# A gated FFN with a masked product, all in fp32: its products done by Strassen's algorithm

## The chip, the cores and the metric

The kernel runs on one core of a Trainium2 chip. The metric is the device time of one execution in microseconds (us), the median of several runs. The engines are TensorE (PE in the profile; PEld is its weight load), VectorE (DVE), ScalarE (ACT), GpSimd (POOL) and SyncE (SP, which here only issues DMAs). Each engine runs its own list of instructions strictly in order and waits on semaphores of the others.

## The reference

There are 2048 tokens (2 x 1024) of 512 features, in fp32. xn is the layernorm of x over its features. The mask is 0 or 1 in blocks of 32 x 32, and a block of the weight is kept where the mask's sum over it is above 0.

```python
xn = _layernorm(x, axis=-1)
s = einsum('bsk,nk->bsn', xn, weight * block_mask)          # 512 x 512
nx = xn * rsqrt(mean(xn * xn) + 1e-5) * ln_w
g = einsum('bsh,ih->bsi', nx, gate_w)                       # 1792 x 512
u = einsum('bsh,ih->bsi', nx, up_w)                         # 1792 x 512
f = einsum('bsi,hi->bsh', silu(g) * u, down_w)              # 512 x 1792
out = x + s * silu(f)
```

## The kernel before

The main loop takes 4 blocks of TB = 512 tokens one after the other. Every product on TensorE is 128 x 128 weights by 128 x 512, in fp32; the profile counts each product written in the code as two instructions. 736 products are written: 224 for gate, 224 for up, 224 for down, 64 for the masked weight.

`prep` (L83 to L128) normalises a block token by token on VectorE (L95 to L113), transposes it on TensorE (L123) and evicts it twice, once times ln_w (L126, VectorE) and once plain (L127, ScalarE). `gate_up` (L143 to L162) then runs over 14 tiles f of the inner dimension: four products into one PSUM bank for gate (L149), four for up (L154), a silu out of PSUM on ScalarE (L158) and one multiplication on VectorE (L160), which makes a tile h that stays in SBUF. `finish` (L164 to L186) runs over 4 tiles of 128 tokens: 14 products with h as the weights of TensorE (L171), 4 of the masked product (L176), silu (L180), two operations on VectorE (L182, L185) and a store (L186). PSUM is accumulated over the contraction: a bank is read once in four, or once in fourteen, products.

All weights are loaded once by SP's queue at the start (L69 to L74) and stay in SBUF. A scheduler orders the instructions of each engine. GpSimd does nothing after it has made the identity matrix. In DRAM lie only inputs and the output.

## Time and profile before

| | |
|---|---|
| median of 3 runs | 658.58 us (658.03 to 659.58) |
| span of the profiled execution | 657.3 us |
| granted TensorE clock, mean | 0.998 |
| first product of gate starts | 12.25 us |
| transposes, 64 instructions of 128x128 (L123) | 10.4 us busy |
| up (L154) and masked product (L176), TensorE busy | 201.4 us and 57.5 us |
| statistics, 16 on VectorE (L95) | 675 ns each |
| eviction by ScalarE, 16 (L127) | 586 ns each |
| DMA over the span | 21.72 MB, 33 GB/s; 424 GB/s in the second of 40 slices |
| a 256 KB load of x, issue to landing | 3.9 us |
| a 256 KB store of the output, issue to landing | 2.0 us |

An engine's busy time alone does not tell what bounds the kernel; the chain of waits, which follows the last instruction back to what released it, does. In a line of a group stand: line, engine, operation, output <- inputs, shapes, count, busy time in us and mean duration in ns, and the idle time of the engine just before these instructions with what ended it. Durations of TensorE's instructions overlap, so they are read from starts. Starts in the timeline are us from the span's start.

### The profile page before, as it was taken

To read this page: it belongs to the slowest core of one execution; us is meant where nothing else is said; L and a number is where in the kernel's file an instruction comes from. 1 tells how busy PE (TensorE), PEld (TensorE's weight loads), DVE (VectorE), ACT (ScalarE), POOL (GpSimd) and SP (SyncE) were. 2 spreads that over 40 slices of the span, in tenths; PEclk is the share of its full clock that TensorE was granted. 3 is DMA by queue.
4 is the path that set the end of the run, shared out by engine and by line. 5 is a ranking of instruction groups with operands and counts; after the bars stand their busy time and mean duration, and the time that the engine had idled before them with its cause. 6 is when DMAs were issued, how large, how long until landed. Compare 5 with 4: busy or idle time off the path is not lost.

```text
span 657.3 us, 3624 instructions
## 1 busy us (share of the span) xinstructions
PE 642.3 (98%) x1538; PEld 288.0 (44%) x1538; DVE 102.0 (16%) x184; ACT 63.5 (10%) x100; POOL 0.7 (0%) x6
## 2 busy tenths in 40 slices
PE   3999999999999999999999999999999999999997
PEld 2444444444444444444444444444444444444442
DVE  5223012200140010200032100120001001010000
ACT  1211101100111001100011010010000000100000
POOL 0000000000000000000000000000000000000000
PEclk9999999999999999999999999999999999999999
DMA  9940000000100000000020000000000000000000
GB/s 324 424 179 0 0 1 0 2 31 16 52 29 0 0 0 1 0 16 17 16 80 1 0 0 1 0 0 17 16 16 16 1 0 0 1 0 0 25 24 16
DMA packets 7359, 21.72 MB, mean 33 GB/s; under 512 B 944, under 2 KB 944, under 8 KB 6832
## 3 DMA queue, kind: packets, MB, share of 16 engines
q1 hardware_dynamic: 7344, 21.50, 8.6%
q8 instruction: 12, 0.20, 0.1%
q14 instruction: 3, 0.02, 0.0%
HBM read 17.30 MB, written 4.19 MB: 33 GB/s over the span
## 4 chain that ended last, share of the span: by engine, by line
PE 98%; DVE 1%; DMA 1%; SPq 0%; issue 0%; ACT 0%; DVEq 0%
PE pg L149 29%; PE py L171 29%; PE pu L154 29%; PE pss L176 8%; PE pt L123 1%; DMA x<-in_x 1%; DVE st L95 0%; SPq L56 0%; DVE o L182 0%; DVE nxT L126 0%; DVE o L185 0%; DVE nz L113 0%; DVE agg L96 0%; ACT root L105 0%; DVE inv L107 0%
## 5 line engine op out<-in xcount | busy, mean ns | idle before, releaser
L149 PE MATMUL pg<-nxT,gate_sb 128*128 128x512 f32 x448 | 202.9, 595 | 0.6 <-DVE nxT L126 0.6
L154 PE MATMUL pu<-nxT,up_sb 128*128 128x512 f32 x448 | 201.4, 592 | 0.0
L171 PE MATMUL py<-down_sb,h 128*128 128x512 f32 x448 | 195.7, 592 | 0.0
L149 PEld LDWEIGHTS pg<-nxT,gate_sb 128*128 128x128 f32 x448 | 85.4, 191 | 107.3 <-issue 106.3
L154 PEld LDWEIGHTS pu<-nxT,up_sb 128*128 128x128 f32 x448 | 85.1, 190 | 107.1 <-issue 107.1
L171 PEld LDWEIGHTS py<-down_sb,h 128*128 128x128 f32 x448 | 84.5, 190 | 103.3 <-issue 103.3
L160 DVE TENSOR_TENSOR h<-sg,pu 128x512 f32<-128x512 f32 x56 | 38.5, 688 | 313.8 <-PE pu L154 313.8
L158 ACT ACTIVATE sg<-pg 128x512 f32<-128x512 f32 x56 | 33.5, 597 | 322.7 <-PE pg L149 322.5
L176 PE MATMUL pss<-w_sb,nzT 128*128 128x512 f32 x128 | 57.5, 592 | 0.0
L182 DVE SCALAR_TENSOR_TENSOR o<-pss,root,g 128x512 f32<-128x512 f32 x16 | 12.0, 751 | 218.5 <-PE pss L176 192.9
L176 PEld LDWEIGHTS pss<-w_sb,nzT 128*128 128x128 f32 x128 | 24.3, 190 | 30.6 <-issue 30.6
L180 ACT ACTIVATE g<-py 128x512 f32<-128x512 f32 x16 | 9.6, 597 | 216.9 <-PE py L171 216.9
L123 PE MATMUL pt<-ident,nz 128*128 128x128 f32 x64 | 10.4, 311 | 9.7 <-DVE nz L113 9.7
L123 PEld LDWEIGHTS pt<-ident,nz 128*128 128x128 f32 x64 | 8.7, 161 | 14.9 <-issue 12.3
L126 DVE TENSOR_SCALAR nxT<-pt,lnw_sb 128x512 f32<-128x512 f32 x16 | 11.4, 745 | 6.1 <-PE pt L123 6.0
L95 DVE BATCH_NORM_STATS2 st<-x 128x6 f32<-128x512 f32 x16 | 10.8, 675 | 9.7 <-DMA x<-in_x 9.7
L127 ACT COPY nzT<-pt 128x512 f32<-128x512 f32 x16 | 9.4, 586 | 25.8 <-DVE nxT L126 25.4
L185 DVE TENSOR_TENSOR o<-o,x 128x512 f32<-128x512 f32 x16 | 11.1, 692 | 0.5
L113 DVE TENSOR_SCALAR nz<-x,agg,scl 128x512 f32<-128x512 f32 x16 | 7.7, 541 | 0.1
L158 ACT ACT_TABLE_LOAD x4 | 5.1, 1283 | 1.6 <-PE pg L149 1.6
L105 ACT ACT_TABLE_LOAD x4 | 5.1, 1283 | 0.8 <-PEq L229 0.7
L96 DVE BATCH_NORM_AGGREGATE agg<-st 128x2 f32<-128x6 f32 x16 | 2.9, 181 | 0.4
(20 smaller groups left out, 11.9 us busy)
## 6 DMA issues: line engine op xcount, KB each, us to landing
x<-in_x SPq DMA_DIRECT2D x16, 256.0 KB, 3.9
out<-o SPq DMA_DIRECT2D x16, 256.0 KB, 2.0
gate_sb<-in_gate_t SPq DMA_DIRECT2D x7, 512.0 KB, 10.0
up_sb<-in_up_t SPq DMA_DIRECT2D x7, 512.0 KB, 10.2
down_sb<-in_down_t SPq DMA_DIRECT2D x2, 1792.0 KB, 17.1
mask_sb<-in_mask_t SPq DMA_DIRECT2D x1, 1024.0 KB, 11.4
w_sb<-in_w_t SPq DMA_DIRECT2D x1, 1024.0 KB, 12.6
lnw_sb<-in_ln_w SPq DMA_DIRECT2D x1, 2.0 KB, 4.0
```

The source lines that it names most:

```text
L95: nc.vector.bn_stats(st, xt[:, t, :])
L123: nc.tensor.transpose(pt[:, t * P : (t + 1) * P], nz[:, t, c * P : (c + 1) * P], ident)
L126: nc.vector.tensor_scalar_mul(nxT[:, c, :], pt, lnw_sb[:, c : c + 1])
L149: nc.tensor.matmul(pg, gate_sb[:, f, c, :], nxT[:, c, :], start=(c == 0), stop=(c == KC - 1))
L154: nc.tensor.matmul(pu, up_sb[:, f, c, :], nxT[:, c, :], start=(c == 0), stop=(c == KC - 1))
L158: nc.scalar.activation(sg, pg, AF.Silu)
L160: nc.vector.tensor_mul(h, sg, pu)
L171: nc.tensor.matmul(py, hs[f][:, tok], down_sb[:, f, :], start=(f == 0), stop=(f == FC - 1))
L176: nc.tensor.matmul(pss, nzT[:, c, tok], w_sb[:, c, :], start=(c == 0), stop=(c == KC - 1))
L180: nc.scalar.activation(g, py, AF.Silu)
L182: nc.vector.scalar_tensor_tensor(o, pss, root[:, TT + t : TT + t + 1], g, ALU.mult, ALU.mult)
L185: nc.vector.tensor_add(o, o, xt[:, t, :])
```

## The change

Strassen's algorithm, in the form with 7 products and 15 sums, replaces 8 products of blocks by 7. With the blocks of A (weights) as A11, A12, A21, A22 and those of B (tokens), the products are numbered 1 to 7; sums of A are named S (outer level) and s (inner level), sums of B T and t.

All 2048 tokens are taken at once, transposed, so that B is 4 x 4 tiles (4 of features by 4 of 512 tokens), A for one `group` is 4 x 4 tiles (two of gate and two of up over 4 of features). A group therefore stands for 64 products, and two levels make it 7 x 7 = 49. There are seven groups for gate and up, and an eighth (g == G) for the masked weight. The outer product q is an `instance`; it consists of 7 inner products. `OUTER = (1, 2, 3, 5, 6, 7, 4)` is their order. Inner product number i of instance j stands at position 7 j + 2 i, so that two instances are always interleaved and each position holds one product. Within an instance some products add into a bank of which a copy or sum was taken before (`start=first`): `snap` reads the bank and TensorE then adds to it, four positions later.

`snap`, `total` and `last` read PSUM after each single product. Where the instance has no earlier sum (q = 1, 3, 5) three snaps and the last are copies on ScalarE and three totals are sums on VectorE; in the others all seven are sums on VectorE. `pool_add` adds the outer sums on GpSimd in SBUF. `done` then runs silu on ScalarE in SBUF and the multiplication that makes h on VectorE, and stores h to DRAM. `sums_of_h` makes the four other blocks that the products of down need, 8 subtractions on VectorE with 8 stores, at position 8.5 of the next group. `inner_a` and `outer_a` make the sums of the weights on GpSimd, into three buffers tagged s and five tagged S; `scale_a` applies ln_w to the weights on ScalarE. The sums of the tokens, T and t, are made once, during the first group, half on VectorE and half on GpSimd (`outer_b`, `inner_b`), and stay in SBUF.

Down is one level: 7 outer products, each over 7 pairs of tiles, 28 products of 128x512 each, 196 in all; a bank is read once in 7 products. The blocks of h are read back from DRAM (`load_h`), 14 tiles of 256 KB for each of the seven, into a pool of 52 buffers shared with the weights of down (`load_d`, `outer_d`), the result of the masked product (also kept in DRAM) and x. Output and a second copy of x are transposed on the host.

`tc.manual_schedule()` keeps every engine's list in the order of the events, which are sorted by position. All DMAs are on SP's queue. Left out of the diff are the removed functions, which stand above, the token statistics (as before in their kind), the mask's reduction (one per quarter, VectorE) and the host's layouts.

```diff
-    ps_gu = ctx.enter_context(tc.tile_pool(name="ps_gu", bufs=4, space=bass.MemoryType.PSUM))
...
+    h_dram = tc.dram_tile([7, G, 2, P, W], F32, name="h_dram")
...
+    bpool = ctx.enter_context(tc.tile_pool(name="bpool", bufs=52))
+    apool = ctx.enter_context(tc.tile_pool(name="apool", bufs=8))
+    cpool = ctx.enter_context(tc.tile_pool(name="cpool", bufs=4))
+    ps = ctx.enter_context(tc.tile_pool(name="ps", bufs=1, space=bass.MemoryType.PSUM))
...
+    PSB = {"X": 3, "Y": 2, "Z": 2, "V": 1}
+    def bank(tag, name):
+        return ps.tile([P, W], F32, tag=tag, name=name, bufs=PSB[tag])
...
+    def transpose(t, c, tag):
+        pt = bank(tag, f"pt_{t}_{c}")
+        for i in range(TT):
+            nc.tensor.transpose(pt[:, i * P : (i + 1) * P], nzs[t][i][:, c * P : (c + 1) * P], ident)
+        r = t2k(bpool, "b", f"raw_{c}_{t}")
+        if c % 2:
+            nc.vector.tensor_copy(r, pt)
+        else:
+            nc.scalar.copy(r, pt)
+        raw[c, t] = r
...
+    def inner_b(q, m, eng):
+        b11, b12, b21, b22 = (bblk[q, k, n] for k in (0, 1) for n in (0, 1))
+        if m == 1:
+            bop[q, 1], bop[q, 2], bop[q, 3] = b11, b21, b22
+            return
+        o = t2k(bpool, "b", f"t{q}_{m}")
+        a, b = {
+            5: lambda: (b12, b11),
+            6: lambda: (b22, bop[q, 5]),
+            7: lambda: (b22, b12),
+            4: lambda: (b21, bop[q, 6]),
+        }[m]()
+        add(eng, o, a, b, ALU.subtract)
+        bop[q, m] = o
...
+    def load_a(g, R, K):
+        a = t2k(apool, "a", f"a{g}_{R}{K}")
+        nc.sync.dma_start(a, gu[g, R, K] if g < G else wm[R, K])
+        aq[g, R, K] = a
+    def scale_a(g, R, K):
+        for c in range(2):
+            v = aq[g, R, K][:, c * 256 : (c + 1) * 256]
+            nc.scalar.mul(v, v, lnw_sb[:, 2 * K + c : 2 * K + c + 1])
...
+    def mask_a(R, K):
+        v = aq[G, R, K].rearrange("p (b j) -> p b j", j=BLK)
+        k = keep[:, 2 * R + K, :].unsqueeze(2).to_broadcast([P, 16, BLK])
+        nc.gpsimd.tensor_tensor(v, v, k, ALU.mult)
+    ablk = {}
+    def outer_a(g, q, eng):
+        if q in (1, 2, 4):
+            ablk[g, q] = aq[(g,) + {1: (0, 0), 2: (0, 1), 4: (1, 1)}[q]]
+            return
+        o = t2k(apool, "S", f"S{g}_{q}", bufs=5)
+        a, b, op = {
+            5: lambda: (aq[g, 1, 0], aq[g, 1, 1], ALU.add),
+            6: lambda: (ablk[g, 5], aq[g, 0, 0], ALU.subtract),
+            7: lambda: (aq[g, 0, 0], aq[g, 1, 0], ALU.subtract),
+            3: lambda: (aq[g, 0, 1], ablk[g, 6], ALU.subtract),
+        }[q]()
+        add(eng, o, a, b, op)
+        ablk[g, q] = o
+    def inner_a(g, q, eng):
+        a = ablk[g, q]
+        a11, a21, a12, a22 = (a[:, i * P : (i + 1) * P] for i in range(4))
+        s = t2k(apool, "s", f"s{g}_{q}", bufs=3)
+        s1, s2, s3, s4 = (s[:, i * P : (i + 1) * P] for i in range(4))
+        add(eng, s1, a21, a22)
+        add(eng, s2, s1, a11, ALU.subtract)
+        add(eng, s3, a11, a21, ALU.subtract)
+        add(eng, s4, a12, s2, ALU.subtract)
+        aop[g, q] = {1: a11, 2: a12, 3: s4, 4: a22, 5: s1, 6: s2, 7: s3}
...
+    def instance(j, g, q, prior, dest):
...
+        def mm(m, tag, key, first):
+            def emit():
+                if first:
+                    st[key] = bank(tag, f"{key}_{j}")
+                nc.tensor.matmul(st[key], aop[g, q][m], bop[q, m], start=first, stop=True, skip_group_check=True)
+            return emit
+        def snap(key, name, i):
+            def emit():
+                s = t2k(cpool, name, f"{name}_{j}", bufs=2)
+                if prior is None:
+                    nc.scalar.copy(s, st[key])
+                else:
+                    add(nc.vector, s, st[key], prior(i))
+                st[name] = s
+            return emit
+        def total(key, name, i, after):
+            def emit():
+                add(nc.vector, dest(i), st[key], st[name])
+                after(i)
+            return emit
+        def last(key, i, after):
+            def emit():
+                if prior is None:
+                    nc.scalar.copy(dest(i), st[key])
+                else:
+                    add(nc.vector, dest(i), st[key], prior(i))
+                after(i)
+            return emit
+        def emit_all(after):
+            plan = (
+                (mm(1, "X", "x", True), snap("x", "s1", 0)),
+                (mm(5, "Y", "y", True), snap("y", "s5", 3)),
+                (mm(6, "X", "x", False), snap("x", "s2", 1)),
+                (mm(2, "Z", "z", True), total("z", "s1", 0, after)),
+                (mm(7, "X", "x", False), total("x", "s5", 3, after)),
+                (mm(3, "Y", "y", False), total("y", "s2", 1, after)),
+                (mm(4, "X", "x", False), last("x", 2, after)),
+            )
+            for i, (product, sums) in enumerate(plan):
+                at(7 * j + 2 * i, product)
+                at(7 * j + 2 * i + 0.5, sums)
+        return emit_all
+    def group(g):
+        base = 7 * 7 * g
...
+        def done(R, Hh, tiles):
+            def after(i):
+                if g == G:
+                    r, n = divmod(i, 2)
+                    t = 2 * Hh + n
+                    nc.gpsimd.tensor_tensor(tiles(i), tiles(i), rms_bc[:, t * W : (t + 1) * W], ALU.mult)
+                    nc.sync.dma_start(s_dram[2 * R + r, t], tiles(i))
+                    return
+                if i < 2:
+                    nc.scalar.activation(tiles(i), tiles(i), AF.Silu)
+                got.setdefault((R, Hh), set()).add(i)
+                for n in (0, 1):
+                    if {n, n + 2} <= got[R, Hh] and (R, Hh, n) not in hs:
+                        nc.vector.tensor_mul(tiles(n), tiles(n), tiles(n + 2))
+                        hs[R, Hh, n] = tiles(n)
+                        q = {(0, 0): 1, (1, 0): 2, (1, 1): 3}.get((R, Hh))
+                        if q:
+                            nc.sync.dma_start(h_dram[q - 1, g, n], tiles(n))
+            return after
+        got, hs = {}, {}
+        def sums_of_h(n):
+            b11, b21, b12, b22 = hs[0, 0, n], hs[1, 0, n], hs[0, 1, n], hs[1, 1, n]
+            T = {}
+            for q in (5, 7, 6, 4):
+                T[q] = t2k(cpool, "T", f"hT{g}_{n}_{q}", bufs=4)
+                a, b = {5: lambda: (b12, b11), 7: lambda: (b22, b12),
+                        6: lambda: (b22, T[5]), 4: lambda: (b21, T[6])}[q]()
+                add(nc.vector, T[q], a, b, ALU.subtract)
+                nc.sync.dma_start(h_dram[q - 1, g, n], T[q])
+        nothing = lambda i: None
+        def pool_add(dst, src):
+            return lambda i: add(nc.gpsimd, dst(i), dst(i), src(i))
+        def chain(*fs):
+            def after(i):
+                for f in fs:
+                    f(i)
+            return after
+        setup = {
+            1: (None, acc_, nothing),
+            2: (acc_, c1_, done(0, 0, c1_)),
+            3: (None, vc_, nothing),
+            5: (None, v5_, pool_add(vc_, v5_)),
+            6: (acc_, acc_, chain(pool_add(vc_, acc_), done(0, 1, vc_))),
+            7: (acc_, acc_, chain(pool_add(v5_, acc_), done(1, 1, v5_))),
+            4: (acc_, acc_, done(1, 0, acc_)),
+        }
...
+        for o, q in enumerate(OUTER):
+            prior, dest, after = setup[q]
+            instance(7 * g + o, g, q, prior, dest)(after)
+        if g < G:
+            at(base + 49 + 8.5, sums_of_h, 0)
+            at(base + 49 + 8.6, sums_of_h, 1)
...
+    def load_h(q):
+        for f in range(G):
+            for n in range(2):
+                hb[q, f, n] = t2k(bpool, "b", f"hb{q}_{f}{n}")
+                nc.sync.dma_start(hb[q, f, n], h_dram[q - 1, f, n])
...
+    def finish(R, Hh, i, y):
+        r, n = divmod(i, 2)
+        t, m = 2 * Hh + n, 2 * R + r
+        s, xx = fin[m, t]
+        nc.scalar.activation(y, y, AF.Silu)
+        nc.vector.tensor_mul(y, y, s)
+        nc.vector.tensor_add(y, y, xx)
+        nc.sync.dma_start(out_t[m * P : (m + 1) * P, t * W : (t + 1) * W], y)
...
+            def products(i=i, tag=tag, r=r, n=n):
+                b = bank(tag, f"py{q}_{i}")
+                for f in range(G):
+                    w = dop[q, f - f % 2][:, (f % 2) * 256 + r * P : (f % 2) * 256 + (r + 1) * P]
+                    nc.tensor.matmul(b, w, hb[q, f, n], start=(f == 0), stop=(f == G - 1))
+                A = lambda d, tag_: tile_of(d, tag_, i)
+                if q == 1:
+                    nc.scalar.copy(A(acc, "acc"), b)
+                elif q == 2:
+                    add(nc.vector, A(c1, "c1"), b, A(acc, "acc"))
+                    finish(0, 0, i, c1[i])
+                elif q == 3:
+                    nc.scalar.copy(A(vc, "vc"), b)
+                elif q == 5:
+                    nc.scalar.copy(A(v5, "v5"), b)
+                    add(nc.gpsimd, vc[i], vc[i], v5[i])
+                elif q == 6:
+                    add(nc.vector, acc[i], b, acc[i])
+                    add(nc.vector, vc[i], vc[i], acc[i])
+                    finish(0, 1, i, vc[i])
+                elif q == 7:
+                    add(nc.vector, acc[i], b, acc[i])
+                    add(nc.vector, v5[i], v5[i], acc[i])
+                    finish(1, 1, i, v5[i])
+                else:
+                    add(nc.vector, acc[i], b, acc[i])
+                    finish(1, 0, i, acc[i])
+            at(base + 28 * o + 7 * i, products)
...
+    at(NEG, load_x, 3)
+    tags = ("X", "Y", "Z", "X", "Y", "Z", "X", "V")
+    for t in (0, 1):
+        at(NEG + 1 + t, norm, t)
+        for c in range(KC):
+            at(NEG + 1 + t, transpose, t, c, tags[4 * t + c])
+    for R, K in QUADS:
+        at(NEG + 1.5, scale_a, 0, R, K)
+    for q in (1, 2):
+        at(NEG + 3, outer_a, 0, q, pool)
+        at(NEG + 3, inner_a, 0, q, pool)
+        for k in (0, 1):
+            for n in (0, 1):
+                at(NEG + 3, outer_b, q, k, n, dve)
+        for m in (1, 5, 6, 7, 4):
+            at(NEG + 3 + (q - 1), inner_b, q, m, dve)
+    at(0.6, norm, 2)
+    at(0.6, norm, 3)
+    for t in (2, 3):
+        for c in (2, 3, 0, 1):
+            at(1.2 + (t - 2) * 4 + 2 * ((c + 2) % 4) / 2, transpose, t, c, "V")
+    for q, pos in ((3, 9.6), (5, 14.6), (6, 21.6), (7, 28.6), (4, 35.6)):
+        for k in (0, 1):
+            for n in (0, 1):
+                at(pos + 0.1, outer_b, q, k, n, pool if (k + n) % 2 else dve)
+        for m in (1, 5, 6, 7, 4):
+            at(pos + 0.2, inner_b, q, m, dve if m in (5, 6, 4) else pool)
+    at(45.6, rms_factor)
+    for g in range(G + 1):
+        base = 49 * g
...
+        if g:
+            for R, K in QUADS:
+                at(base - 40, load_a, g, R, K)
+            for i, (R, K) in enumerate(QUADS):
+                if g < G:
+                    at(base - 24 + 2 * i + 0.7, scale_a, g, R, K)
+                else:
+                    at(base - 24 + 2 * i + 0.7, mask_a, R, K)
+            for q in (1, 2):
+                at(base - 15 + 7 * (q - 1) + 0.8, outer_a, g, q, pool)
+                at(base - 15 + 7 * (q - 1) + 0.9, inner_a, g, q, pool)
+        for i, q in enumerate((5, 6, 3, 7, 4)):
+            at(base - 7.1 + 2 * i, outer_a, g, q, pool)
+        for o, q in enumerate(OUTER[2:]):
+            at(base + 7 * o + 2.8, inner_a, g, q, pool)
+    for i, (R, K) in enumerate(QUADS):
+        at(49 * 4 + 6 * i + 0.75, mask_rows, R, K)
+    END = 49 * (G + 1) + 6
+    for i, (R, K) in enumerate(((0, 0), (1, 0), (1, 1), (0, 1))):
+        at(END - 14 + i, load_d, R, K)
+    for q in (1,):
+        at(END - 10, outer_d, q, pool)
+    for q in (2, 5, 6, 3, 7, 4):
+        at(END - 0.5, outer_d, q, pool)
+    at(END - 10, load_h, 1)
+    for o, q in enumerate(OUTER):
+        if o:
+            at(END + 28 * (o - 1) - 0.1, load_h, q)
+        quad = {2: (0, 0), 6: (0, 1), 7: (1, 1), 4: (1, 0)}.get(q)
+        if quad:
+            at(END + 28 * (o - 1) + 0.1, prefetch_out, *quad)
+        last_product(o, q, END)
...
+    with tc.manual_schedule():
+        for _, _, fn, args in sorted(events, key=lambda e: e[:2]):
+            fn(*args)
```

## The prediction, made before the changed kernel had run

> **What bounds the kernel now.** I read the chain of waits first, then the groups of instructions, then the timeline around the places where the change puts its work.
>
> ```profile
> PE 642.3 (98%) x1538; PEld 288.0 (44%) x1538; DVE 102.0 (16%) x184; ACT 63.5 (10%) x100; POOL 0.7 (0%) x6
> PE 98%; DVE 1%; DMA 1%; SPq 0%; issue 0%; ACT 0%; DVEq 0%
> L149 PE MATMUL pg<-nxT,gate_sb 128*128 128x512 f32 x448 | 202.9, 595 | 0.6 <-DVE nxT L126 0.6
> L171 PE MATMUL py<-down_sb,h 128*128 128x512 f32 x448 | 195.7, 592 | 0.0
> ...
> L160 DVE TENSOR_TENSOR h<-sg,pu 128x512 f32<-128x512 f32 x56 | 38.5, 688 | 313.8 <-PE pu L154 313.8
> L158 ACT ACTIVATE sg<-pg 128x512 f32<-128x512 f32 x56 | 33.5, 597 | 322.7 <-PE pg L149 322.5
> ...
> L185 DVE TENSOR_TENSOR o<-o,x 128x512 f32<-128x512 f32 x16 | 11.1, 692 | 0.5
> ```
>
> TensorE is the whole chain; everybody else waits for it. A written product is two instructions (448 for 224). In the chain in order of time 28 of them take 12.02 us, so a product costs 0.859 us, and 736 of them 632 us of the 657.3 us span. Prices of the other engines come from these lines:
>
> ```profile
> 128.89 12.02 PE py L171 x28
> ```
> ```profile
> 101.05 3.60 PE L154 MATMUL pu<-nxT,up_sb 128*128 128x512 f32 x8
> 104.75 0.69 DVE L160 TENSOR_TENSOR h<-sg,pu 128x512 f32<-128x512 f32 x1 [6.18 <-PE pu L154]
> 652.64 0.75 DVE L182 SCALAR_TENSOR_TENSOR o<-pss,root,g 128x512 f32<-128x512 f32 x1 [13.97 <-PE pss L176]
> 653.42 0.69 DVE L185 TENSOR_TENSOR o<-o,x 128x512 f32<-128x512 f32 x1
> ```
> ```profile
> 0.24 0.10 POOL L229 MEMSET const-float32-0.0<- 128x1 f32 x1 [0.24 <-issue]
> 0.73 0.20 POOL masks.py:197 MEMSET ident<- 128x128 f32 x1 [0.29 <-POOLq L229]
> 1.01 0.29 POOL masks.py:199 TENSOR_SCALAR_AFFINE_SELECT ident<-ident 128x128 f32<-128x128 f32 x1
> ```
>
> A result can be read 0.26 us after the next product starts (104.75 against 101.05 + 4 x 0.859 = 104.49), so 1.12 us after its own start. A 128x512 VectorE operation is 0.69 us, 0.03 us from a dependent one; I count 0.68 in a full queue. A ScalarE pass is 0.60, each hop between engines 0.07 (estimate, half of the hops seen).
>
> **What is taken away.** 343 products for gate and up, 49 for the mask, 196 for down: 588 against 736. 148 x 0.859 = 127.1 us less on TensorE, which is the chain. If nothing else changed: 530 us.
>
> **What is added, per group of 49 products** (seven groups for gate and up, one for the mask; 42.1 us of TensorE each). VectorE: 37 sums out of PSUM, 8 multiplications for h, 8 subtractions in `sums_of_h`: 53 x 0.69 = 36.6 us. GpSimd: 12 `pool_add` and 4 `outer_a` of 128x512, 28 adds of 128x128. No row shows a two-input GpSimd add. Overhead 0.10, writing 128 elements 0.10 more, reading one input as well 0.09 more; a second input at the same step gives 0.385 us for 128 elements and 0.10 + 4 x 0.285 = 1.24 us for 512. Bounds: 0.88 (one input only, 0.10 + 4 x 0.195) and 1.76 (two such passes). I take 1.24, the step that the rows show. 16 x 1.24 + 28 x 0.385 = 30.6 us. ScalarE: 12 copies and 8 silus of 0.60, 8 half tiles of 0.4 (between 0.60 for 512 elements and 0.21 for 8): 15 us. So by busy time each engine fits under 42.1. It is the order that costs: every engine runs its list in order, and VectorE's list mixes sums that free PSUM with multiplications that wait for GpSimd.
>
> I followed one group by hand; times in us from the start of its product 20, products numbered 0 to 48, product 49 being 0 of the next group. A product may start when the sum that reads its bank, four products earlier in the same instance, is done.
>
> 1. The sum after product 38 ends at 17.2. Next in VectorE's order is the h multiplication of vc1, which waits for its silu, which waits for GpSimd's `vc1 += acc1`. GpSimd has run `inner_a` of instance 4 until 12.5 and three adds until 16.3; then stands `inner_a` for the next group, whose s tile (3 buffers) is free only after product 38: to 18.3. Two adds: 20.8. Silu 21.5, multiplication 22.2. Behind it stands the sum after product 39, ending 22.9, on whose bank product 43 waits: 22.95 for 19.7. Stall 3.2.
> 2. The next multiplication waits for `vc2 += acc2` in the same way and ends at 25.6; two sums later, at 27.0, product 46 may start, not at 25.5. Stall 1.5.
> 3. VectorE reaches the multiplication of v51 at 29.0. GpSimd, from 26.4: v50 add 27.6, `inner_a` 29.3, S5 30.6, v53 31.8, S6 33.0, v51 34.3. Silu 35.0, multiplication 35.7, sum after product 46 36.4: product 50 at 36.5 for 30.5. Stall 6.0.
> 4. The first sum of instance 4 (product 48) ends at 39.8. Its silu stands on ScalarE ahead of the copy that product 53 waits for: 41.2 for 39.0. Stall 2.2.
> 5. The eight subtractions (5.5 us) stand between the sums after products 56 and 58: product 61 at 49.6 for 48.1, product 64 at 54.4 for 52.1. Stalls 1.5 and 2.3.
>
> Sum 16.7: a group takes 58.8 us. After product 64 VectorE catches up, so each group begins the same. On this path lie nine 128x512 and eight 128x128 GpSimd adds: at 0.88 (0.295) the group is 54.8, at 1.76 (0.59) about 65.
>
> Two costs are not in it. TensorE starts slowly after idling: its first eight transposes take 1.97 us, four of them 0.61 later at work, 0.25 against 0.15 each, and the profile's granted clock is full in both.
>
> ```profile
> 9.65 1.97 PE L123 MATMUL pt<-ident,nz 128*128 128x128 f32 x8 [9.65 <-DVE nz L113]
> 111.51 0.61 PE L123 MATMUL pt<-ident,nz 128*128 128x128 f32 x4
> ```
>
> After stalls of 3 and 6 us that could return: nothing, or some three products at most 0.86 dearer, 2.6. And whether GpSimd and VectorE slow each other when both are busy, no row shows, since GpSimd is idle here; nothing to a few tenths for each of 16 operations. I take 1.3 for both together: 60.0 us per group. The Trainium skill (TensorE: Matmul & The Clock Gate, Loop structure matters more than you think) warns against idle gaps over about 3 us, after which the array runs at half clock; that agrees with the slow start, and by it the full 2.6 would be paid, 8 us more in all. The skill (GPSIMD Engine Reference, Engine selection) speaks against this change: elementwise sums belong on VectorE, GpSimd being about 2x slower. It gives 4497 ns for an add of 2048 elements; a quarter is an estimate of 1.12 us, by which the whole sum would be some 7 us less.
>
> **Start.** Before, product 0 starts at 12.25 us. Now two blocks of tokens come first: the second repeats statistics (4 x 0.86), small operations (0.9), normalisation on ScalarE (4 x 0.60), 16 transposes at 0.25 and copies: product 0 at 25.4. Then TensorE's order has the transposes of blocks 2 and 3, which wait for VectorE: 8 subtractions (5.5) and two times 4.3 of statistics, to 40.4; normalisation to 42.9; then seven turns of the one V bank at 1.5 us (transposes 0.6, copy 0.6, hops): product 9 at 53.7.
>
> **Sum, from the span.** 53.7 to product 9. To product 20 of group 1: 60 x 0.859 = 51.5, one set of stalls 16.7, 23 subtractions for T and t on a VectorE with no slack 15.9: 137.8. Six groups of 60.0: 497.8. Last group: no h, so VectorE never waits for silu; GpSimd's 20 late operations (24.8 us) trail behind; 35 products 30.1, and mask sums earlier 2: 529.9. Change to down: its weights and first h come on SP's queue behind stores that wait for GpSimd. From that store (12 us after product 34) 30 loads at 0.62 us (256 KB at 424 GB/s), the last needed at 30.8, product row done at 31.5 for 24: 7.5. Down: 196 x 0.859 = 168.3. Tail: sum 0.69, silu 0.7, two operations 1.4, store 3.2 as now, hops 0.5: 6.5. Span 712.2; the median shown lies 1.3 above the span: **713.5 us**.
>
> Costed at nothing: h through DRAM. Eighteen transfers of 256 KB in 60 us are 79 GB/s; in down 38 MB in 168 us are 228 GB/s, against 424 at the start. TensorE hides them; at half that speed down takes 13 us more. The stores wait for VectorE, and behind them on SP stand the next group's weights, needed 14 us later. `scale_a` (3.2 us per group) lies under ScalarE's 27 idle us; without that cover, 3.2 per group.
>
> **Rivals.**
> - TensorE stays the bound: results wait in PSUM and every stall is covered, as the busy times 36.6 and 30.6 under 42.1 suggest. 505 for products, 46 of start, 16 in group 0, 7.5 and 6.5, 1.3: **582 us**. Against it: VectorE's order has the multiplication ahead of the sum that frees the bank. Chance 0.07.
> - Half the stalls: GpSimd is fast enough that only the silu and the subtractions are felt, 50.5 per group: **648 us**. It needs a GpSimd add at VectorE's 0.69 or less. 0.07.
> - GpSimd bound: adds at 1.76, a group at 66.3, group 0 nine more: **760 us**. 0.12.
> - Down starved by loads: 726 us, within the forecast's own range.
> - That it does not do what it says: the product counts are fixed by the loops; no chance given.
>
> **How the numbers follow.** The forecast, groups held up by VectorE waiting for GpSimd, has 0.74, its likeliest time 713. At 0.88 us per add and no slow clock it is 676, at the full clock cost and 1.5 us 745. Range 672 to 756, which leaves out the two fast rivals and the end of the slow one. Faster by over 0.2% 0.14, within 0.2% (what a measurement here can tell) 0.01, slower 0.85.
>
> **What would show it.** In the profile after: `h` multiplications (their line in `done`) with idle time before them released by ACT or POOL, some 12 us per group; GpSimd adds near 1.24 us start to start; TensorE about 70% busy in the first two thirds and full in the last quarter; a group every 60 us. If those multiplications wait for little, or groups come every 43 us, the forecast is wrong.

## The result, and the profile after

The changed kernel takes 778.16 us (772.79 to 783.28) against 659.08 beside it: 1.181 times as long, 95% interval 1.175 to 1.187. The forecast was 713 (672 to 756). The direction was right; the time lies 22 us beyond the range. The profiled execution has a span of 778.8 us, and the forecast's sum for it was 712.2, so 66.6 us have to be found.

The page of the kernel after: busy time of each engine, the chain of waits by engine, one group of GpSimd's outer additions, and from the list of groups the two multiplications that make h out of the second quarter (`vc`) and the third (`v`).

```profile
PE 590.2 (76%) x1248; PEld 251.0 (32%) x1248; DVE 375.2 (48%) x568; ACT 149.3 (19%) x269; POOL 336.8 (43%) x416
...
PE 49%; DVE 18%; POOL 15%; issue 7%; DMA 6%; ACT 3%; SPq 1%; DVEq 0%; POOLq 0%; ACTq 0%
...
L77 POOL TENSOR_TENSOR v<-v,acc 128x512 f32<-128x512 f32 x32 | 40.5, 1266 | 24.8 <-DVE acc L77 24.8
...
L336 DVE TENSOR_TENSOR v<-v,v 128x512 f32<-128x512 f32 x14 | 19.7, 1406 | 53.5 <-ACT v L332 43.8
...
L336 DVE TENSOR_TENSOR vc<-vc,vc 128x512 f32<-128x512 f32 x14 | 9.7, 692 | 39.8 <-ACT vc L332 30.2 <-POOL vc L77 9.6
```

TensorE was 98% of the chain and is 49% now. No engine is full; VectorE and GpSimd, both under half busy, hold a third of the chain between them. That is an order that waits, not an engine that is short of time.

The next view cuts the span into windows of 60 us: busy time and instructions (x) of PE, PEld, DVE, ACT and POOL, then the granted TensorE clock, the DMA share and GB/s.

```profile
60.00:120.00 60.00, 38.06 (x70) 15.29 (x70) 41.79 (x50) 10.81 (x21) 42.76 (x45) 0.83 0.03 9
...
240.00:300.00 60.00, 47.86 (x98) 19.51 (x98) 36.36 (x53) 14.16 (x28) 32.96 (x44) 0.91 0.21 79
300.00:360.00 60.00, 28.97 (x52) 12.35 (x53) 26.71 (x41) 6.48 (x11) 18.94 (x22) 0.74 0.23 83
...
660.00:720.00 60.00, 60.00 (x141) 26.60 (x140) 6.71 (x10) 5.36 (x9) 5.06 (x4) 1.00 0.71 247
```

A steady window holds 98 instructions of TensorE, which is 49 products, one group; TensorE works 48 of its 60 us. Between 300 and 360 us only 52 start. In down (the last row) TensorE is full. So there are three things to explain: the pace of a steady group, one hole of about 30 us, and a slow beginning.

Products are numbered by their positions, as in the forecast. Measured from product 23 of one group to product 23 of the next, where TensorE runs at its own pace, the seven intervals from group 0 on are, by TensorE's starts: 88.7 (into group 1), then 62.2, 61.4, **91.4**, 62.5, 61.6 and 64.5 us.

**The steady group.** TensorE's rows between two such points; the bracket is what a product waited for.

```profile
394.44 2.05 PE L262 MATMUL x<-t,s 128*128 128x512 f32 x2 [3.05 <-DVE s L77]
396.27 1.92 PE L262 MATMUL y<-t,s 128*128 128x512 f32 x2
397.98 1.91 PE L262 MATMUL y<-T,s 128*128 128x512 f32 x2
399.69 1.43 PE L262 MATMUL x<-t,s 128*128 128x512 f32 x2
400.96 1.02 PE L262 MATMUL x<-t,S 128*128 128x512 f32 x2
...
409.20 2.05 PE L262 MATMUL x<-t,s 128*128 128x512 f32 x2 [5.51 <-DVE s L77]
411.04 1.91 PE L262 MATMUL y<-t,s 128*128 128x512 f32 x2
412.75 1.73 PE L262 MATMUL y<-T,s 128*128 128x512 f32 x2
...
422.78 1.12 PE L262 MATMUL x<-t,a 128*128 128x512 f32 x2 [1.02 <-DVE acc L77]
...
427.99 2.08 PE L262 MATMUL x<-t,s 128*128 128x512 f32 x2 [2.37 <-DVE s L77]
429.86 1.70 PE L262 MATMUL y<-t,s 128*128 128x512 f32 x2
```

A product that waits for nothing starts 0.859 us after the one before. Two kinds of loss are seen. The waits, each product's delay against that step: 3.21, 5.67, 1.19 and 2.53 us, 12.6 in all, at products 43, 50, 61 and 64, four of the six that the forecast named. And what comes behind them: after 394.44 the next starts are 1.83, 1.71, 1.71 and 1.27 us apart, although nothing is waited for. That is 3.1 us; it is 2.9 behind 409.20 and 1.7 behind 427.99: 7.7 us of slow restart. Together 20.3 us over the 42.1 of 49 products at full pace. The granted clock goes with it: the windows view gives 0.53 from 394.40 to 400.90 us, and 1.00 from 241.60 to 247.00, in another group, where the products go on at full pace behind the same idle time of 3.05 us.

**The hole.** Rows of TensorE, VectorE and SP around the first of the four small mask products (`pm`). SPq rows are DMA issues.

```profile
314.85 1.07 DVE L336 TENSOR_TENSOR v<-v,v 128x512 f32<-128x512 f32 x1 [5.92 <-ACT v L332]
...
315.95 4.63 SPq L340 DMA_DIRECT2D h_dram<-v  x2
...
318.50 1.73 DVE L336 TENSOR_TENSOR v<-v,v 128x512 f32<-128x512 f32 x1 [1.38 <-POOL v L77]
...
320.63 0.42 SPq L212 DMA_DIRECT2D mask<-in_mask  x1
...
323.39 0.69 DVE L214 TENSOR_REDUCE rows<-mask 128x16 f32<-128x512 int32 x1 [2.56 <-DMA mask<-in_mask]
...
324.23 0.58 PE L216 MATMUL pm<-rows,blockones 128*128 128x16 f32 x2 [13.47 <-DVE rows L214]
...
324.64 2.05 PE L262 MATMUL x<-t,s 128*128 128x512 f32 x2
```

Read it from the bottom. `pm` stands in TensorE's list and waits 13.47 us for the mask's row sums. VectorE's reduction waits for the mask's load. The load was issued at 320.63, because ahead of it in SP's queue stand two stores of h (315.95 and behind it), the second of which waits for the multiplication at 318.50, and that for GpSimd. So one event (load, reduce, product, all at the same position) stopped three queues. It happens four times; in the list of waits the four cost TensorE 32.0 us (the first stands where product 50 would have waited some 6 us without it):

```profile
PE pm L216 <- DVE rows L214: 32.0, 4, 13.5
...
DVE rows L214 <- DMA mask<-in_mask: 13.0, 4, 4.6
```

**The beginning.** SP's queue in group 0; `rms_dram<-rms` stores 2048 single numbers, `rms_bc` reads them back.

```profile
124.94 0.37 SPq L159 DMA_DIRECT2D rms_dram<-rms  x1
135.78 0.33 SPq L160 DMA_DIRECT2D rms_bc<-rms_dram  x1
136.21 0.38 SPq L340 DMA_DIRECT2D h_dram<-v  x1
136.68 1.14 SPq L340 DMA_DIRECT2D h_dram<-acc  x2
137.91 9.81 SPq L354 DMA_DIRECT2D h_dram<-hT  x8
```

The read waits 10.8 us for the store to land (the list of DMAs gives 10.8 us from issue to landing for its 8 KB, beside 2.0 for a store of 256 KB). Everything behind it waits too: the eight stores of hT begin at 137.91, the four hT buffers come free late, and VectorE, which frees PSUM in the same list, stands 5.62 us before the fifth subtraction (144.59).

### The profile page after: what moved, and what is told of

It is laid out like the page before. It is cut to its first block, busy times and chain, and to the rows that moved or that the text cites. A ratio compares the mean times of both kernels' runs of the same rounds, so it can differ in the third digit from the quotient of the medians.

```text
span 778.8 us, 4884 instructions
## 1 busy us (share of the span) xinstructions
PE 590.2 (76%) x1248; PEld 251.0 (32%) x1248; DVE 375.2 (48%) x568; ACT 149.3 (19%) x269; POOL 336.8 (43%) x416
## 4 chain that ended last, share of the span: by engine, by line
PE 49%; DVE 18%; POOL 15%; issue 7%; DMA 6%; ACT 3%; SPq 1%; DVEq 0%; POOLq 0%; ACTq 0%
PE py L451 21%; PE x L262 14%; PE y L262 9%; POOL vc L77 5%; DVE acc L77 3%; POOL s L77 3%; POOL v L77 3%; DVE hT L77 3%; PE z L262 3%; DVE s L77 3%; DVE t L77 3%; POOL S L77 2%; DMA h_dram<-hT 2%; DMA mask<-in_mask 2%; PE pt L139 1%
## 5 line engine op out<-in xcount | busy, mean ns | idle before, releaser
L262 PE MATMUL x<-t,s 128*128 128x512 f32 x224 | 135.7, 691 | 82.0 <-DVE s L77 81.3
L451 PE MATMUL py<-hb,dS 128*128 128x512 f32 x224 | 96.3, 592 | 0.0
L262 PEld LDWEIGHTS x<-t,s 128*128 128x128 f32 x224 | 45.2, 216 | 152.1 <-issue 124.4
L451 PE MATMUL py<-hb,d 128*128 128x512 f32 x168 | 75.3, 608 | 10.4 <-DMA hb<-h_dram 10.4
L262 PE MATMUL y<-t,s 128*128 128x512 f32 x112 | 72.6, 736 | 0.0
L451 PEld LDWEIGHTS py<-hb,dS 128*128 128x128 f32 x224 | 42.6, 190 | 53.6 <-issue 52.4
L77 POOL TENSOR_TENSOR v<-v,acc 128x512 f32<-128x512 f32 x32 | 40.5, 1266 | 24.8 <-DVE acc L77 24.8
L77 POOL TENSOR_TENSOR vc<-vc,acc 128x512 f32<-128x512 f32 x32 | 40.3, 1266 | 20.8 <-DVE acc L77 20.7
L77 POOL TENSOR_TENSOR vc<-vc,v 128x512 f32<-128x512 f32 x32 | 40.4, 1270 | 18.1 <-DVE v L77 18.1
L77 DVE TENSOR_TENSOR s<-x,acc 128x512 f32<-128x512 f32 x64 | 44.1, 689 | 7.9 <-PE x L262 3.5
L336 DVE TENSOR_TENSOR v<-v,v 128x512 f32<-128x512 f32 x14 | 19.7, 1406 | 53.5 <-ACT v L332 43.8
L139 PE MATMUL pt<-ident,nz 128*128 128x128 f32 x64 | 16.7, 397 | 30.8 <-ACT nz L126 26.6
L262 PE MATMUL x<-t,a 128*128 128x512 f32 x48 | 26.4, 632 | 11.9 <-DVE acc L77 9.4
```

The costliest lines, as they stand in the source:

```text
L77: eng.tensor_tensor(o, a, b, op)
L139: nc.tensor.transpose(pt[:, i * P : (i + 1) * P], nzs[t][i][:, c * P : (c + 1) * P], ident)
L262: nc.tensor.matmul(st[key], aop[g, q][m], bop[q, m], start=first, stop=True, skip_group_check=True)
L336: nc.vector.tensor_mul(tiles(n), tiles(n), tiles(n + 2))
L451: nc.tensor.matmul(b, w, hb[q, f, n], start=(f == 0), stop=(f == G - 1))
```

## The experiments

Eleven kernels. Each builds on an earlier one; along the line e1, e4, e5, e7, e8, e11 the differences can be added. Ratios are to the kernel before, with a 95% interval.

**e1: the mask's sums one step ahead.** The event is cut in three, the load 10 positions before the reduction and that 8 before the product, once for each quarter, and all of it earlier, the load by 30 to 72 positions and the product by 12 to 54.

```diff
-        at(49 * 4 + 6 * i + 0.75, mask_rows, R, K)
+        at(49 * 2 + 26 + 20 * i + 0.75, mask_load, R, K)
+        at(49 * 2 + 26 + 20 * i + 10.75, mask_sum, R, K)
+        at(49 * 2 + 26 + 20 * i + 18.75, mask_rows, R, K)
```

> The changed kernel with one thing moved: each quarter of the mask is loaded, reduced on VectorE and multiplied on TensorE at three positions far apart, a group earlier, instead of at one. Theory A (in that group TensorE stands 5 to 13.5 us four times because its next instruction needs a mask that SP has not asked for yet, SP being behind stores that wait for VectorE): group 3 to 4 falls from 91 us to about 62, time 778 to about 749. Theory B (the group is long because VectorE has four more reductions, or because of the lower clock): 4 x 0.69, at most 5 us, time 773 or more.

Measured: 746.08 us (744.61 to 750.01), ratio 1.133 (1.129 to 1.137), 32.1 us less than the change as made. All intervals from group 1 on are now 59 to 63 us; the 91.4 is gone. The hole was the place of the mask event and not its work, which is still done.

**e2: no work for h.** e1 without the silus, without the h multiplications and without the eight subtractions; the stores stay and write other tiles, so h is not what the reference computes.

```diff
-                if i < 2:
-                    nc.scalar.activation(tiles(i), tiles(i), AF.Silu)
...
-                        nc.vector.tensor_mul(tiles(n), tiles(n), tiles(n + 2))
...
-                add(nc.vector, T[q], a, b, ALU.subtract)
+                T[q] = {5: b11, 7: b12, 6: b22, 4: b21}[q]
```

> As the run with the mask ahead, with silu, the h multiplications and the eight subtractions per group left out; the stores and their places stay, but store unfinished tiles, so h and the output are not the reference's. Theory A (VectorE stands in its order behind GpSimd and ScalarE, and behind the subtractions): groups of about 45 us for 62, time about 749 - 7 x 17 = 630. Theory B (the granted clock of 0.87 is imposed from elsewhere): groups of at least 42.1 / 0.87 = 48 us, the clock still near 0.87, time 650 or more. Theory C (GpSimd is the bound): groups stay at 55 or more.

Measured: 615.81 us (one run, so without an interval), groups of 42.5 to 44.7 us. With every PSUM sum, every GpSimd addition and every transfer still there, TensorE runs nearly at its own pace of 42.1. So the loss of a steady group, some 18 us, is tied to 24 operations of h; the 37 sums and GpSimd's load by themselves do not limit it. Since 16 of them are 11 us of VectorE, this alone does not yet tell their work from their place. A clock imposed from elsewhere falls as the cause: the mean granted clock is 0.952 here and 0.897 in e1, so it is higher where less is waited for.

**e3: a fourth s buffer** (and one S buffer less), so that `inner_a` for the next group need not wait for product 38.

```diff
-        s = t2k(apool, "s", f"s{g}_{q}", bufs=3)
+        s = t2k(apool, "s", f"s{g}_{q}", bufs=4)
-        o = t2k(apool, "S", f"S{g}_{q}", bufs=5)
+        o = t2k(apool, "S", f"S{g}_{q}", bufs=4)
```

> As the run with the mask ahead, with four s buffers for three (one S buffer fewer, which pays for it). Theory A (in the first long stall GpSimd stands before inner_a for a buffer that TensorE still reads, and the add that VectorE waits for stands behind it): the stall at product 43 falls from 3.2 by about 1.7 us, a group from 62 to 60, time 749 to about 737. Rival (GpSimd has idle time enough, it only waits at another place): within 3 us of the run with the mask ahead.

Measured: 741.41 us (740.27 to 746.75), ratio 1.1257 (1.1214 to 1.1300); the intervals overlap with e1's 1.133 at their edges (1.129, 1.130). Groups take 59 to 61.6 us. The wait at product 43 went from 3.20 to 2.89 only; the others are as in e1, at product 50 some 6 us. The buffer is a small part. What holds the sum for product 43 up in its place stays open.

**e4: the same h work, later.** From e1: silu and multiplication become events of their own, each placed some positions after the GpSimd addition that it reads, so that VectorE and ScalarE have it in their lists when it can run. Nothing is left out.

```diff
-                if i < 2:
-                    nc.scalar.activation(tiles(i), tiles(i), AF.Silu)
...
+        for R, Hh, tiles, s0, s1, m1, m0 in (
+            (0, 0, c1_, 13.6, 17.6, 19.6, 21.6),
+            (0, 1, vc_, 38.6, 45.6, 46.6, 48.6),
+            (1, 1, v5_, 47.6, 54.6, 55.6, 57.3),
+            (1, 0, acc_, 48.6, 52.6, 54.55, 56.6),
+        ):
+            if g < G:
+                at(base + s0, silu, tiles, 0)
+                at(base + s1, silu, tiles, 1)
+                at(base + m1, mul, R, Hh, tiles, 1)
+                at(base + m0, mul, R, Hh, tiles, 0)
```

> As the run with the mask ahead, with silu and the h multiplications placed later in the order of ScalarE and VectorE (up to ten products), where GpSimd's add should be done; same instructions. Theory A (the order costs, not the work): the stalls at products 43, 46, 50 and 53 (together about 13 us of a group) shrink to a few us, groups of 50 to 53 us, time about 680. Theory C (VectorE and GpSimd together have too much work, or slow each other in SBUF): groups of 60 or more, time above 735.

Measured: 686.96 us (686.35 to 688.55), ratio 1.042 (1.0402 to 1.0438): 59.1 us less than e1, groups of 51.5 to 54.2. The list of waits (total us, times, longest) for the sums that free PSUM, first in e1, then in e4:

```profile
PE x L270 <- DVE s L77: 90.8, 25, 8.5
```
```profile
PE x L270 <- DVE s L77: 12.3, 4, 7.1
```

The work is the same and the wait fell from 90.8 to 12.3 us. That for sums into `acc`, among them those behind the subtractions, rose from 18.5 to 41.9 meanwhile (18.4 in e5, which takes these on). This tells work from place: the place costs. It is the step on which the forecast rested.

**e5: the eight subtractions one by one** instead of in two blocks of four, from e4.

```diff
-            at(base + 49 + 8.5, sums_of_h, 0)
-            at(base + 49 + 8.6, sums_of_h, 1)
+            for n, q, pos in ((0, 5, 8.6), (0, 7, 9.6), (0, 6, 10.6), (0, 4, 11.6),
+                              (1, 5, 14.6), (1, 7, 15.6), (1, 6, 17.6), (1, 4, 18.6)):
+                at(base + 49 + pos, sum_of_h, n, q)
```

> As the run with the late multiplications, with the eight subtractions of a group no longer in one burst behind position 8 of the next group but one by one between positions 8 and 19; same instructions. Theory A (VectorE's burst holds back the sums that free the banks; the late-multiplication run still stands 4.5 us at product 57 and restarts slowly): groups from 52 to 46 or 47 us, time 687 to about 652. Theory C (the subtractions cost VectorE's time wherever they stand): groups stay at 51 or more, time above 680.

Measured: 657.96 us (656.28 to 659.79), ratio 0.9975 (0.9963 to 0.9987): 29.0 us less than e4, groups of 48 to 51 us, and level with the kernel before.

**e6: the RMS factor later.** From e1: computed at 49 + 24.6, its root, store and read at 49 + 36.6, away from the stores of hT.

```diff
-    at(45.6, rms_factor)
+    at(49 + 24.6, rms_factor)
+    at(49 + 36.6, rms_root)
```

> As the run with the mask ahead, with the RMS factor of the masked product (its small operations, root and the store and load of its 2048 numbers) moved from the end of group 0 into group 1, where SP has nothing to store. Theory A (the store of 2048 single numbers takes 10.7 us on SP's queue, the stores of the subtractions stand behind it, and VectorE waits for their buffers; TensorE stands 7.7 us at product 61 of this one group, against 2 elsewhere): 6 to 8 us less, about 739. Rival (TensorE's stall there is the burst alone): within 2 us of 746.

Measured: 732.77 us (732.04 to 739.31), ratio 1.1122 (1.1074 to 1.1170), 13.3 us less than e1 where 6 to 8 were expected; the profiled execution is the slowest of the four (739.31). In its trace product 23 of group 0 to product 23 of group 1 is 78.4 us (e1: 89.1), 10.7 less. Product 64 is delayed by 2.18 us (e1: 8.70), product 50 by 6.08 (e1: 8.23). The groups behind are as in e1.

**e7: all of it.** e5, e3 and e6 together, and GpSimd's list put in the order of need: `outer_a` and `inner_a` for the next group stand behind the additions that h waits for, and the silus and multiplications of vc and v5 in e4's table move up to four positions ahead with them.

```diff
-            for q in (1, 2):
-                at(base - 15 + 7 * (q - 1) + 0.8, outer_a, g, q, pool)
-                at(base - 15 + 7 * (q - 1) + 0.9, inner_a, g, q, pool)
+            for q, pos in ((1, 40.8), (2, 48.1)):
+                at(base - 49 + pos, outer_a, g, q, pool)
+                at(base - 49 + pos + 0.05, inner_a, g, q, pool)
...
-            at(base - 7.1 + 2 * i, outer_a, g, q, pool)
+            at((base - 0.8 if g else -7.1) + 0.05 * i, outer_a, g, q, pool)
...
-            at(base + 7 * o + 2.8, inner_a, g, q, pool)
+            at(base + 7 * o + (4.8 if g else 2.8), inner_a, g, q, pool)
```

> Late multiplications, spread subtractions, four s buffers and the later RMS factor together, and in GpSimd's order the sums that h waits for ahead of the weight sums for the next group. Theory A (only order and buffers hold TensorE up): groups of 43 to 45 us, as where h was left out (43.5), and time about 625, less than before the change. Theory C (with h in it, VectorE and GpSimd have too much work): groups of 48 or more, time above 645.

Measured: 632.53 us (629.77 to 634.52), ratio 0.9591 (0.9567 to 0.9615), groups of 45 to 47 us: between the two expectations, nearer the first.

**e8: the start.** From e7: block 2's statistics during block 1, the transposes of blocks 2 and 3 in two alternating banks, one per position from 4.2, and the sums T and t spread from position 13.

```diff
-            at(1.2 + (t - 2) * 4 + 2 * ((c + 2) % 4) / 2, transpose, t, c, "V")
+    for i, (t, c) in enumerate(((2, 2), (2, 3), (3, 2), (3, 3), (2, 0), (2, 1), (3, 0), (3, 1))):
+        at(4.2 + i, transpose, t, c, "VZ"[i % 2])
```

> As the run before it, with the start rearranged: the first 10 products need token blocks 0 and 1 only, so the transposes of blocks 2 and 3 come after the first of them and alternate between two banks, and the sums T and t of group 0 are spread out and start earlier. Theory A (TensorE's order, with transposes that wait ahead of products that do not, costs some 23 us before product 9, and group 0 waits for the T of GpSimd): product 9 at about 35 us for 54, group 0 some 10 us shorter, time about 597. Rival (the start is bound by VectorE's statistics and subtractions, whatever the order): at most 10 us less, time above 613.

Measured: 613.18 us (612.79 to 614.83), ratio 0.9293 (0.9279 to 0.9307), 19.4 us less than e7. About half of what was expected at the start came: product 9 starts at 45.5 us, not 35 (e7: 54.4). TensorE still waits 7.5 us at product 4 (35.91 us) for a copy on ScalarE, which stands there behind a square root for the next block, and that waits 9.5 us for VectorE's statistics.

**e9: GpSimd's outer additions on VectorE.** From e1, so with the order of the change as made: another way to take GpSimd out of VectorE's waits.

```diff
-            return lambda i: add(nc.gpsimd, dst(i), dst(i), src(i))
+            return lambda i: add(nc.vector, dst(i), dst(i), src(i))
```

> e1 with the twelve outer additions of a group (pool_add) on VectorE instead of GpSimd, everything else in the same order. Theory (VectorE's list waits for GpSimd): the h multiplications then wait only for a silu, four times 0.75 us per group; VectorE's own list is 65 operations of 0.69, 44.9 us, so a group takes about 48 to 52 us where e1 takes 61.5, and the time is about 665. Rival 1 (VectorE is nearly full already, and 8 us more per group on it cost what the waits save): 740 to 750, a group 60. Rival 2 (the pace is that of TensorE restarting slowly, whatever releases it): groups of 57 to 60, about 730.

Measured: 698.48 us (697.23 to 700.40), ratio 1.0598 (1.0571 to 1.0626): 47.6 us less than e1, groups of 54 to 57 us where 48 to 52 were expected. The direction is that of the theory and both rivals fall, but a third of a group's loss of 19.3 us went, not half or more. What is left: waits of 1.9, 1.3, 3.4, 1.4 and 2.2 us in one group. Ahead of the longest of them VectorE took 1.79 us for one of the additions moved to it (timeline of e9, GpSimd and VectorE at that place), and then waited for the silu behind it:

```profile
289.66 1.26 POOL L77 TENSOR_TENSOR S<-S,a 128x512 f32<-128x512 f32 x1
289.68 1.79 DVE L77 TENSOR_TENSOR v<-v,acc 128x512 f32<-128x512 f32 x1
...
291.00 1.59 POOL L77 TENSOR_TENSOR S<-a,S 128x512 f32<-128x512 f32 x1
```

**e10: the same edit on e8**, where TensorE's list of waits names GpSimd no more.

> e8 with the twelve outer additions of a group on VectorE. In e8 nothing waits for GpSimd in a steady group any more (45.1 to 47.9 us per group against 42.1 for TensorE alone). Theory: VectorE's busy time rises from 36.6 to 44.9 us per group, which is above TensorE's 42.1, so groups take 46 to 49 and the time is 613 to 630, no better than e8. Rival (the slowing of VectorE beside GpSimd is what keeps e8 from 42.1): groups of 44, about 600.

Measured: 636.69 us (634.31 to 638.44), ratio 0.9656 (0.9626 to 0.9686): 23.5 us more than e8 and 7 above the upper end expected; groups of about 50 us. The group of VectorE that was moved there:

```profile
L77 DVE TENSOR_TENSOR vc<-vc,acc 128x512 f32<-128x512 f32 x32 | 35.2, 1101 | 1.1
```

VectorE got the additions of this group at 1.10 us each, not 0.69; those of the other two took 0.77 and 0.74. GpSimd still works beside it, the likely reason (see the last section). The three groups moved (35.2, 24.7 and 23.8 us) make 10.5 us in each of eight groups, and VectorE is busy 43 to 46 us of a group's 49 to 50. It is not alone: TensorE's list of waits now has 14.9 us, at eight places, for GpSimd's sums of weights.

**e11: down's loads ahead of the last stores.** From e8.

```diff
-        at(END - 14 + i, load_d, R, K)
+        at(END - 24 + i, load_d, R, K)
-    at(END - 10, load_h, 1)
+    at(END - 19, load_h, 1)
```

> e8 with the loads of down's weights and first h moved 10 and 9 positions ahead in SP's list, so that they stand ahead of the last twelve stores of s, which wait for GpSimd. Theory: the 9.8 us of TensorE's idle time before down is the queue's order; down starts some 8 us earlier, about 605. Rival (the buffers that these loads go into are freed by the last products, so the order does not matter): 613, and the stores of s land later.

Measured: 607.01 us (604.27 to 608.34), ratio 0.9220 (0.9197 to 0.9243). TensorE's 9.8 us of idle time before down went to about nothing: the last product starts at 422.45, down at 423.41. This version beats both kernels. Its page, in busy time and in the chain of waits:

```profile
PE 538.7 (89%) x1248; PEld 234.5 (39%) x1248; DVE 382.9 (64%) x568; ACT 146.9 (24%) x269; POOL 366.6 (61%) x416
...
PE 63%; DVE 19%; POOL 8%; issue 4%; ACT 3%; DMA 3%; DVEq 0%; SPq 0%; POOLq 0%; ACTq 0%
```

It has the instructions of the change as made, x for x; only their order and the number of s and S buffers differ. It is 171 us shorter (778.16 - 607.01).

## Why the prediction was right in kind and wrong in size

The wait that the forecast is built on, VectorE's list standing behind GpSimd, is there. What failed is the step "mask sums earlier 2", the RMS store that no term had, and the size of two terms: the slow restart, and T and t.

Where the 66.6 us lie, by TensorE's starts: product 9 at 54.4 for 53.7 (0.7); from there to product 20 of group 1, 102.0 for 84.1 (17.9); six groups 403.7 for 360.0 (43.7); from there to the end 218.7 for 214.4 (4.3).

- **What is taken away** held: 1248 instructions less the 72 of transposes and mask are 588 products, and at full pace 0.859 us each.
- **Prices.** A GpSimd addition of 512 took 1.27 us, 1.22 from start to start (forecast 1.24), one of 128 elements 0.46 in the three quickest groups of them, 0.73 in the slowest (0.385). The rule weighed in the prediction, that sums belong on VectorE, is true of one order and false of the other: moving them saved 47.6 us in e9 and cost 23.5 in e10.
- **VectorE's list waiting for GpSimd** held, and e2, e4 and e9 show it. VectorE stands idle before the two multiplications shown for 53.5 and 39.8 us in seven groups, 13.3 per group, where some 12 were forecast. The stalls were at the products named: 3.2, 1.5, 6.0, 2.2, 1.5 and 2.3 forecast; 3.21, none, 5.67, none to speak of, 1.19 and 2.53 in the group shown above. The second is swallowed by a slow restart: in the three groups whose products go on at full pace behind product 43 it is there, 1.42, and the third is 6.08 in two of them; in the other the hole follows. The fourth falls within the slow restart behind product 50 in every group.
- **The slow restart** was mis-sized. "I take 1.3 for both together" halved a cost of 2.6 us and gave it once per group; in the group shown it is 7.7 us in three places. The forecast read a full granted clock beside the slow first transposes; behind the waits here the slow products go with a granted clock of 0.53. With the waits at 12.6 instead of 16.7, the group takes 62.4 by this sum for 60.0, and 61.4 to 64.5 by the intervals without the hole: 15 us over six groups. That 60.0 came so near is in part luck: 4.1 us too much for the waits stood against 6.4 too little for the restart. The page named there (TensorE: Matmul & The Clock Gate; the bound is in its table under Why this matters for your kernels), by which the full cost would be paid, was nearer in size, but its bound of about 3 us is not what the trace shows: in this group the restart is slow behind idle times of 5.51, 3.05 and 2.37 us, and in three other groups (at 241.64, 303.02 and 456.93) products go on at full pace behind the same 3.05. No run takes the restart away and leaves the wait, so its share is read from starts, not tried.
- **"Mask sums earlier 2"** is the step that failed most. The forecast gave the mask 2 us, the size of its work on the engines, and followed SP's queue for the weights only, not for the mask's loads. The wait is in three queues at once (SP behind h stores, VectorE behind the load, TensorE behind VectorE): 29 us in that group's interval (91.4 against 62.2), 32.1 in the median by e1.
- **Group 0 and 1.** From product 9 to product 43 TensorE lost 26.4 us against its pace, where 15.9 were forecast for T and t: 10.5 more. VectorE's 23 subtractions took 25.5 us there, ten of them 1.19 to 1.75 each and not 0.69, with GpSimd at work on the others beside them; one waited 2.92 for GpSimd, and TensorE restarts slowly behind each of the long waits. No run tells these apart. From product 43 to product 20 of group 1 it lost 24.1, where one set of stalls, 16.7, was forecast: 7.4 more. That is the RMS factor, which no term had: 2048 numbers take 10.8 us to land and hold SP's queue. In e6 the same stretch loses 13.8.
- **Last group, change to down, down, tail:** 218.7 for 214.4. The last group took 30.8 us for 30.1 and the mask's 2: from product 20 on there are 32 products, not 35 (three positions are empty at the end), and the last of them waits 3.14 for VectorE. The way to down took 10.1 for 7.5, of which 9.86 are the wait for the first h. Down took 171.6 for 168.3, the tail 6.2 for 6.5. "h through DRAM, costed at nothing" held: in down TensorE is full at 247 GB/s.
- **The rivals.** GpSimd as the bound falls: it is 43% busy, and waits on TensorE and VectorE. Half the stalls falls with the price of an addition, 1.27 for the 0.69 or less that it needed, and down starved by loads with the full TensorE in down. "TensorE stays the bound", 582, is no description of this order, but e2 and e11 show that it is what the same instructions come near to when the lists are in the order of need: of the 116 us by which e1's groups exceed TensorE's own time over six groups (61.4 less 42.1, times 6), e8's groups of 45.1 to 49.0 leave 24.

Added up from medians: mask 32.1, h work at its place 59.1, subtractions 29.0, buffers with RMS and GpSimd's order 25.4, start 19.4, loads 6.2: from 778.2 to 607.0.

## What to carry to other kernels

In a kernel whose lists are ordered by hand, an instruction that waits for another engine must not stand ahead of the one that frees the bound engine's buffer; put it where its input is already there, and split an event of load, reduction and product into three places. Before a step is costed at nothing, follow it through every queue that it stands in, the DMA queue first: what is issued ahead of it there, and what that waits for. In this case the sign of such an order was that no engine was full, and that two engines under half busy held a third of the chain; 171 us were to be had without removing a single instruction.

## What the runs showed of the hardware

- After a wait of 5 us and more, TensorE's next products start 1.84, 1.71 and 1.71 us apart instead of 0.859, 2.7 us in all, in fp32. Behind 3.05 us of idle time it did so in some groups and not in others (granted clock 0.53 and 1.00 over the products behind it), and behind 2.02 to 2.79 us ahead of product 64 in each of the five groups where that was the wait.
- VectorE's multiplication of two SBUF tiles took 0.69 us alone and 1.73 beside a GpSimd addition (the `v<-v,v` at 318.50; mean 1.406 of 14), while sums with one input in PSUM stayed at 0.68 to 0.69 in the means of their groups. This agrees with the Trainium skill (SBUF — State Buffer, Who interferes with whom): a VectorE instruction with two SBUF inputs and a GpSimd instruction that reads SBUF contend for ports that one of them holds alone, and one with a single SBUF input is left alone. Both sides pay: in e9 a GpSimd addition beside such an instruction took 1.59 and 1.71 us for 1.27.
- VectorE's independent additions out of PSUM start 0.60 us apart though each lasts 0.68 (315.85 and 316.45 us in the trace after).
- A store of 8 KB as 2048 single numbers took 10.8 us to land, a store of 256 KB in long rows 2.0.
